# Layer 3 of a graph network: 22 full steps from up to two chunks each, instead of 42 steps of one chunk

## The chip, the core and the metric

The kernel runs on one core of one Trainium2 chip. The metric is the time on the device in microseconds (us), the median of several executions. A core has TensorE (PE; matmuls, results go to banks of PSUM memory), VectorE (DVE), ScalarE (ACT; functions such as exp and ln), GpSimd (POOL; here it issues the gathers) and SyncE (SP; here it issues the plain loads), and 16 DMA engines[...]. Each engine runs its own instructions in a fixed order, and waits on semaphores for those of the others.

## The reference

Four graph layers on 2708 nodes with 128 features and a dense 0/1 matrix adj of 2708 x 2708. Each layer is x = x + layer(relu(layernorm(x)), adj). The change concerns the fourth:

```python
def _L3_gnn_ref(X, A, W, a):
    XW = jnp.matmul(X, W)
    f = W.shape[1]
    s_col = jnp.matmul(XW, a[0, :f])
    s_row = jnp.matmul(XW, a[0, f:])
    Z1 = jax.nn.leaky_relu(s_row[:, None] + s_col[None, :], negative_slope=0.01)
    den = jnp.exp(Z1)
    num = jnp.matmul(A, den)
    att = jnp.where(num != 0, den / jnp.where(num != 0, num, 1.0), 0.0)
    H = jnp.matmul(A, jnp.matmul(att, XW))
    return H
```

So num is a product of two 2708 x 2708 matrices, of which the second, den, is built from one number for each row (r = s_row) and one for each column (c = s_col).

## The kernel before

Layers 0 to 2 stream the adjacency matrix through TensorE in 22 tiles of 128 rows (the rows of the page with line L209). They end at about 443 us and the change leaves them alone. Everything is float32 unless noted; a float32 matmul shows in the trace as two records.

Layer 3 doesn't form num by a full product. It sorts the nodes by r and cuts them into NC = 22 chunks of CH = 126 nodes. A column with the value c meets the bend of the leaky relu, r + c = 0, inside one chunk. For the nodes of all lower chunks and of all higher ones the leaky relu is linear, so their exp factors into a number of the node and one of the column: two prefix sums over the sorted nodes stand for them. num of one column is therefore a sum over 128 terms: the 126 nodes of its chunk and two prefix rows. The columns are grouped by their chunk, and one step takes up to 128 columns of one chunk. As each chunk's count is rounded up to full steps, the loop has a fixed NS = (2708 + 22 x 127) // 128 = 42 steps (L425), many with few columns or none.

**The tables** (L501 to L772, about 443 to 589 us) are built on the chip, since they depend on the data. First the rank of each node (L555 to L602). Then:

- sums(t) (L626): prefix sums of the adjacency. adj_t is streamed in 22 tiles of 128 rows into the four buffers of the pool steps (tag rows); the first two tiles go into dflat. Six matmuls a tile (L635). Its result goes through hn to a table pre_d in device memory (L778 to L786).
- ktab (L655 to L662): for each chunk the r and the number of its nodes, by a one-hot matmul.
- many (L684 to L688): how many columns each chunk has; pre (L674): how many columns of the same chunk come before each column.
- place, pos, step, slot (L697 to L709): the step of each column and its place in it. ohp and jrhs are the one-hot factors of the matmul L716, which collects, for each step, c (c_tab), the node number (xw_i) and exp(c) (c_exp).
- sel and pick (L732 to L747): for each step its chunk, hence which rows of adj_t (row_i) and of pre_d (pre_i) to gather, and r_step.
- densities(s0) (L749), for four steps at a time: dmat, the 128 x 128 matrix exp(leaky(r + c)) of each step. TensorE spreads c over the partitions (L761), VectorE adds r and applies the slopes, ScalarE the exp. dmat lies in dflat.

**The loop** (L808 to L826). fetch(s) (L793) gathers the 126 rows of the chunk from adj_t and two rows from pre_d into one of the four buffers of steps, and the projected features of the step's columns (fetch_xw, L457) into one of four xw_s. All gathers are issued by POOL, in order. Then, for each of six blocks b of up to 512 nodes, L817 computes num for 128 columns into a PSUM bank (there are two, L83), ScalarE takes its Ln (L818), VectorE subtracts it (L820) from e, which L813 set to the exponent of den without its linear part. After the six blocks ScalarE takes the exp of e (L822): this is att, but for factors of the row and the column. spread_values(s - 1) (L803) then multiplies the step before: six matmuls L806 of xw and e, collected over all steps in six PSUM banks. e and ln have two buffers (L788). Ln and exp need different ACT tables, so that each step shows two table loads.

**What sets the order.** The Tile framework schedules: [...] work may stand earlier than where the code has it. A pool's buffer is handed out again when its last reader is done.

After the loop the result is turned and scaled (L829 to L836), and a last product with adj_t (L860) ends the kernel; it streams adj_t into the buffers of steps and three more.

## Time and profile before

| | us |
|---|---|
| median of 3 runs | 1143.9 (1142.64 to 1145.51) |
| the profiled execution, as run | 1146.82 |
| its span, first to last instruction | 1145.0 |
| layers 0 to 2 | 0 to about 443 |
| tables of layer 3 | about 443 to 613 |
| loop, first L817 to last L806 | 613.32 to 1035.04 |
| last product | 1035.9 to the end |
| busy: PE, DVE, ACT, POOL | 1058.6, 557.5, 587.8, 260.0 |
| mean granted TensorE clock | 0.972 of full speed |

The page lists groups of instructions by line, engine, operation and tiles. The busy share of an engine is a mean over stages with different limits; what an edit is worth is read in its own stage. The chain of waits follows the last instruction back to what released it. In the timeline, each row gives the start, the duration, the engine, the line, the operation, and in brackets the idle time before it and what ended it. Both kernels print the same way, so the stages can be laid side by side.

### The profile page before, as it was taken

How to read it: one execution, taken by the hardware profiler on the slowest of the kernel's cores; microseconds unless marked ns; L12 is line 12 of the kernel's file. 1: busy time of each engine (PE TensorE's matmuls, PEld its weight loads, DVE VectorE, ACT ScalarE, POOL GpSimd, SP SyncE). 2: the span in 40 equal slices, each digit the busy share in tenths (PEclk: the TensorE clock that was granted, in tenths of full speed). 3: DMA queues.
4: the chain of work that ended last, by engine and by line, in shares of the span. 5: the costliest groups of instructions: out<-in, count | busy, mean ns of one | idle time of the engine just before them, and what ended most of it. 6: DMA issues, size and time to landing. Idle time of an engine off the chain costs nothing.

```text
span 1145.0 us, 8681 instructions
## 1 busy us (share of the span) xinstructions
PE 1058.6 (92%) x3110; PEld 464.3 (41%) x3110; DVE 557.5 (49%) x910; ACT 587.8 (51%) x682; POOL 260.0 (23%) x172
## 2 busy tenths in 40 slices
PE   5799999999999997759985999999999999999998
PEld 3333333444545444424421344444444444445444
DVE  5899999410131014884953455545554445542001
ACT  4689673210040003670014888888888888880000
POOL 3000001100110001100212455555555555500000
PEclk9899999999999998888998999999999999999999
DMA  8165544488647805302985344444444444647851
GB/s 320 68 250 212 188 158 125 158 302 304 223 195 260 309 14 209 134 1 107 369 316 188 129 150 153 152 153 152 145 139 140 144 147 152 188 159 317 306 210 48
DMA packets 36684, 211.64 MB, mean 185 GB/s; under 512 B 8234, under 2 KB 17114, under 8 KB 17874
## 3 DMA queue, kind: packets, MB, share of 16 engines
q1 hardware_dynamic: 21223, 146.96, 34.5%
q0 software_dynamic: 9408, 61.00, 16.2%
q10 hardware_dynamic: 6011, 3.14, 1.1%
q8 instruction: 24, 0.39, 0.1%
q14 instruction: 18, 0.15, 0.0%
HBM read 207.77 MB, written 3.32 MB: 184 GB/s over the span
## 4 chain that ended last, share of the span: by engine, by line
PE 28%; ACT 23%; DMA 2%; DVE 1%; issue 1%; DVEq 0%; POOLq 0%
PE bank L817 11%; PE acc L209 9%; ACT e L822 9%; ACT ln L818 6%; ACT L818 4%; ACT L822 4%; PE acc L635 4%; DMA rows<-in_adj_t_dram 2%; PE acc L806 1%; PE bank L761 1%; PE bank L185 1%; PE acc L660 0%; PE acc L716 0%; DMA xw<-xw_d,xw_i 0%; DVE e L820 0%
## 5 line engine op out<-in xcount | busy, mean ns | idle before, releaser
L817 PE MATMUL bank<-rows,dflat 128*128 128x512 f32 x504 | 218.8, 564 | 25.7 <-ACT ln L818 16.0
L806 PE MATMUL acc<-e,xw 128*128 128x512 f32 x504 | 198.0, 542 | 2.1 <-ACT e L822 2.1
L820 DVE TENSOR_TENSOR e<-e,ln 128x1536 f32<-128x1536 f32 (+2 forms) x126 | 134.6, 1097 | 109.4 <-ACT ln L818 104.9
L818 ACT ACTIVATE ln<-bank,tiny 128x512 f32<-128x512 f32 x252 | 151.5, 634 | 57.7 <-PE bank L817 57.2
L817 PEld LDWEIGHTS bank<-rows,dflat 128*128 128x128 f32 x504 | 83.3, 190 | 157.8 <-ACT ln L818 118.0
L450 POOL DMA_INDIRECT xw<-xw_d,xw_i x42 | 90.6, 2157 | 238.6 <-PE acc L806 150.7
L806 PEld LDWEIGHTS acc<-e,xw 128*128 128x128 f32 x504 | 93.0, 190 | 103.1 <-issue 90.4
L813 DVE TENSOR_SCALAR e<-row_a,c_rel 128x2708 f32<-128x2708 f32 x42 | 68.5, 1630 | 99.9 <-PE acc L806 99.8
L822 ACT ACTIVATE e<-e 128x2708 f32<-128x2708 f32 x42 | 103.3, 2460 | 1.7 <-DVE e L820 1.2
L209 PE MATMUL acc<-rows,hn 128*128 128x512 f32 (+1 forms) x264 | 101.7, 542 | 0.0
L209 PE MATMUL acc<-a,hn 128*128 128x512 f32 (+1 forms) x264 | 100.9, 542 | 0.0
L204 ACT COPY yT<-acc 128x512 f32<-128x512 f32 x9 | 5.2, 581 | 178.4 <-PE acc L209 174.9
L450 POOL DMA_INDIRECT rows<-pre_d,pre_i x42 | 89.9, 2140 | 29.7 <-DMA pre_d<-hn 17.2
L209 PE MATMUL acc<-a,hs 128*128 128x512 f32 (+1 forms) x228 | 88.1, 542 | 0.0
L286 ACT ACTIVATE tau<-row_a,e_neg,e_lo 128x1536 f32<-128x1536 f32 (+1 forms) x44 | 65.0, 1509 | 36.5 <-PE bank L301 26.6
L301 PE MATMUL bank<-tau,pick 128*6 128x512 f32 x180 | 72.6, 542 | 0.0
L209 PEld LDWEIGHTS acc<-a,hn 128*128 128x128 f32 x264 | 47.0, 190 | 50.2 <-issue 50.2
L209 PEld LDWEIGHTS acc<-rows,hn 128*128 128x128 f32 x264 | 46.8, 190 | 49.0 <-issue 48.8
L209 PE MATMUL acc<-yT,hs 128*128 128x512 f32 x132 | 57.2, 571 | 7.8 <-DVE yT L292 7.8
L289 DVE SCALAR_TENSOR_TENSOR tau<-tau,e_hi,a 128x1536 f32<-128x1536 f32 (+1 forms) x38 | 60.5, 1622 | 3.0 <-ACT tau L286 3.0
L209 PEld LDWEIGHTS acc<-a,hs 128*128 128x128 f32 x228 | 41.2, 190 | 45.4 <-issue 45.4
L635 PE MATMUL acc<-rows,wts 128*44 128x452 f32 (+1 forms) x240 | 55.0, 581 | 3.7 <-DMA rows<-in_adj_t_dram 3.7
(263 smaller groups left out, 1056.4 us busy)
## 6 DMA issues: line engine op xcount, KB each, us to landing
rows<-in_adj_t_dram SPq DMA_DIRECT2D x40, 1354.0 KB, 7.5
a<-in_adj_dram SPq DMA_DIRECT2D x38, 1354.0 KB, 6.4
a<-in_adj_t_dram SPq DMA_DIRECT2D x21, 1354.0 KB, 6.2
keep<-in_adj_dram SPq DMA_DIRECT2D x2, 1354.0 KB, 5.7
dflat<-in_adj_t_dram SPq DMA_DIRECT2D x2, 1354.0 KB
xw_d<-hs ACTq DMA_DIRECT2D x1, 1408.0 KB
row_a<-rdeg_d ACTq DMA_DIRECT2D x1, 1354.0 KB
xs<-in_x_dram SPq DMA_DIRECT2D x5, 256.0 KB
```

The lines of the kernel that those rows point to most:

```text
L209: nc.tensor.matmul(accs[b][:, : hi - lo], stationary, moving[:, lo:hi], start=start, stop=stop)
L286: nc.scalar.activation(tau[:, :w], row_a[:, h0:h1], AF.Relu, bias=e_neg[:, t : t + 1], scale=e_lo[:, t : t + 1])
L289: nc.vector.scalar_tensor_tensor(tau[:, :w], tau[:, :w], e_hi[:, t : t + 1], a[:, h0:h1], ALU.add, ALU.mult)
L301: nc.tensor.matmul(den[: len(E0), : hi - lo], pick[:, b, :], tau[:, lo - h0 : hi - h0], start=(ndone == 0), stop=(t == T - 1 and b == NB - 1),
L450: return nc.gpsimd.indirect_dma_start(out=out, out_offset=None, in_=src, in_offset=bass.IndirectOffsetOnAxis(ap=idx, axis=0),)
L635: nc.tensor.matmul(accs[b][64 * h : 64 * h + 2 * NC, : hi - lo], wts[:, t, :], a[:, lo:hi], start=(t == 0), stop=(t == T - 1),)
L806: nc.tensor.matmul(accs[b][:, : hi - lo], xw, e[:, lo:hi], start=(s == 0), stop=(s == NS - 1))
L813: nc.vector.tensor_scalar(e, row_a[:, :N], c_rel[:, s : s + 1], 0.0, ALU.add, ALU.max)
L817: nc.tensor.matmul(num[:, : hi - lo], dmat[:, s, :], a[:, lo:hi], start=True, stop=True)
L818: nc.scalar.activation(ln[:, lo:hi], num[:, : hi - lo], AF.Ln, bias=tiny)
L820: nc.vector.tensor_sub(e[:, beg:hi], e[:, beg:hi], ln[:, beg:hi])
L822: nc.scalar.activation(e, e, AF.Exp)
```

## The change

The columns are packed into NE = 22 steps which are all full (128 x 22 = 2816 places for 2708 columns), and a step takes columns from up to two chunks: one that has a step of its own, and one taken from a row in which the columns of the large chunks are laid end to end. So each step needs two row sets, and num is the sum of two matmuls into the same bank, one for each chunk. Where a column isn't of the chunk, its density is made zero: its c in c_two is -3.0e4, and exp gives 0. The table code gets the packing: which chunks are small or large (donor), in which order they come (key, order), and where their columns go (shift_b, past). It is all on VectorE, on rows of 22 or tables of 22 x 22 elements (row, gathered, sums_before). There are now 44 dmat matrices (NS = 2 NE), for which dflat grows, but 22 columns in the tables of steps. krhs moves to yT and sel to hT, many is computed ahead of pre, and one more column block (chunk1) goes through the one-hot matmul. The loop runs 22 times: two fetches, one fetch_xw, 12 matmuls L817, the same six Ln, one exp and six matmuls L806 as before. The pools are as they were: four buffers for rows, two banks, two of e.

In the changed file the lines of the loop move: L716 becomes L809, L761 becomes L875, L817 becomes L933, L806 becomes L918, L818 becomes L936, L822 becomes L940.

```diff
--- before.py
+++ after.py
@@ -420,9 +420,16 @@
     CH = P - 2
     NC = T
-    NS = (N + NC * (P - 1)) // P
+    NE = T
+    NS = 2 * NE
     c_col, r_col = hs[:, :, P], hs[:, :, P + 1]
     xw_d = dram.tile([NPAD, D], F32, name="xw_d")
@@ -436,14 +443,14 @@
         pools.append(pools.pop(0))
         return fill(pool.tile([P, N], F32, tag="rows", name="rows"), src, t)
-    dflat = keepers.tile([P, 2 * N], F32, name="dflat")
+    dflat = keepers.tile([P, max(2 * N, NS * P)], F32, name="dflat")
     dmat = dflat[:, : NS * P].rearrange("p (s q) -> p s q", q=P)
...
@@ -652,7 +659,7 @@
...
-        krhs = tab.tile([P, T, 2 * NC], F32, tag="w1", name="krhs")
+        krhs = yT[:, : T * 2 * NC].rearrange("p (t b) -> p t b", b=2 * NC)
         nc.vector.tensor_mul(krhs[:, :, :NC], ohc, over(r_of, NC))
         nc.vector.tensor_mul(krhs[:, :, NC:], ohc, over(node_v, NC))
         p = acc_bank(3)
@@ -671,6 +678,11 @@
         nc.vector.memset(gej[:, :, NC], 0.0)
         nc.vector.tensor_tensor(gej[:, :, 1:NC], over(negc, NC - 1), along(edges[:, 1:], NC - 1), ALU.is_ge)
         ohb = tt("ohb", [P, T, NC], gej[:, :, :NC], gej[:, :, 1:], ALU.subtract, BF16)
+        p = acc_bank(3)
+        for t in range(T):
+            nc.tensor.matmul(p[:, :NC], ones_b, ohb[:, t, :], start=(t == 0), stop=(t == T - 1))
+        many = tab.tile([P, NC], F32, name="many")
+        nc.vector.tensor_copy(many, p[:, :NC])
         pre = acc_bank(5)
         nc.tensor.matmul(pre[:, : T * NC], before, ohb.rearrange("p t b -> p (t b)"), start=True, stop=False)
         for t in range(T - 1):
@@ -681,70 +693,172 @@
                 start=False,
                 stop=(t == T - 2),
             )
-        p = acc_bank(3)
-        for t in range(T):
-            nc.tensor.matmul(p[:, :NC], ones_b, ohb[:, t, :], start=(t == 0), stop=(t == T - 1))
-        many = tab.tile([P, NC], F32, name="many")
-        nc.vector.tensor_copy(many, p[:, :NC])
...
+        def row(name, n=NC):
+            return tab.tile([P, n], F32, name=name)
+        def square(x):
+            return x[:, :, None].to_broadcast([P, NC, NC])
+        def square_t(x):
+            return x[:, None, :].to_broadcast([P, NC, NC])
+        def gathered(name, m, x):
+            v = tt("sq_v", [P, NC, NC], m, square_t(x), ALU.mult, tag="w3")
+            o = row(name)
+            nc.vector.tensor_reduce(o, v, AX.X, ALU.add)
+            return o
+        def sums_before(name, x):
+            o = row(name)
+            nc.vector.tensor_tensor_scan(o, ones[:, :NC], x, 0.0, ALU.mult, ALU.add)
+            nc.vector.tensor_sub(o, o, x)
+            return o
...
+        d_key = sums_before("d_key", d_over)
+        s_key = sums_before("s_key", s_over)
+        d_idx = sums_before("d_idx", donor)
+        head = row("head")
+        nc.vector.scalar_tensor_tensor(head, d_idx, 0.0, donor, ALU.is_equal, ALU.mult)
...
+        key = row("key")
+        nc.vector.tensor_mul(key, d_key, donor)
+        nc.vector.tensor_sub(key, key, head)
...
+        n_row = row("n_row")
+        nc.vector.tensor_mul(n_row, many, inrow)
+        n_own = row("n_own")
+        nc.vector.tensor_sub(n_own, many, n_row)
+        nc.vector.scalar_tensor_tensor(key, key, 2.0, donor, ALU.mult, ALU.add)
+        nc.vector.scalar_tensor_tensor(key, key, 32.0, lane[:, :NC], ALU.mult, ALU.add)
+        ahead = tt("ahead", [P, NC, NC], square(key), square_t(key), ALU.is_gt, tag="ohc")
+        order = row("order")
+        nc.vector.tensor_reduce(order, ahead, AX.X, ALU.add)
+        row_beg = gathered("row_beg", ahead, n_row)
+        own_before = gathered("own_before", ahead, n_own)
+        far_down = float(1 << 16)
+        own_beg = row("own_beg")
+        nc.vector.tensor_scalar(own_beg, order, -1.0, float(P), ALU.add, ALU.mult)
+        row_at = row("row_at")
+        nc.vector.tensor_sub(row_at, own_beg, own_before)
...
         place = tt(
-            "place", [P, T, NC], pre[:, : T * NC].rearrange("p (t b) -> p t b", b=NC), along(s_off, NC), ALU.add, tag="w3")
...
+        at = row("at", T)
+        nc.vector.tensor_reduce(at, place, AX.X, ALU.add)
+        past = tt("past", [P, T, NC], over(at, NC), along(row_at, NC), ALU.is_ge, tag="w3")
+        nc.vector.tensor_mul(past, past, along(n_own, NC))
+        pos = row("pos", T)
+        nc.vector.tensor_reduce(pos, past, AX.X, ALU.add)
...
+        chunk1 = row("chunk1", T)
+        nc.vector.tensor_reduce(chunk1, gej[:, :, :NC], AX.X, ALU.add)
+        gs = tt("gs", [P, T, NE + 1], over(pos, NE + 1), along(by_p, NE + 1), ALU.is_ge, tag="w1")
+        ohst = tt("ohst", [P, T, NE], gs[:, :, :NE], gs[:, :, 1:], ALU.subtract, tag="w2")
+        step = row("step", T)
         nc.vector.tensor_reduce(step, gs[:, :, 1:], AX.X, ALU.add)
...
         nc.vector.tensor_tensor(ohp, along(lane, P), over(slot, P), ALU.is_equal)
-        jrhs = row_b[:, : T * 3 * NS].rearrange("p (t s) -> p t s", s=3 * NS)
-        nc.vector.tensor_mul(jrhs[:, :, :NS], ohst, over(c_col, NS))
-        nc.vector.tensor_mul(jrhs[:, :, NS : 2 * NS], ohst, over(node_v, NS))
-        nc.vector.tensor_mul(jrhs[:, :, 2 * NS :], ohst, over(w_col, NS))
+        jrhs = row_b[:, : T * 4 * NE].rearrange("p (t s) -> p t s", s=4 * NE)
+        for i, v in enumerate((c_col, node_v, w_col, chunk1)):
+            nc.vector.tensor_mul(jrhs[:, :, i * NE : (i + 1) * NE], ohst, over(v, NE))
         p = acc_bank(4)
         for t in range(T):
-            nc.tensor.matmul(p[:, : 3 * NS], ohp[:, t, :], jrhs[:, t, :], start=(t == 0), stop=(t == T - 1))
...
+        c_chunk = row("c_chunk", NE)
+        nc.vector.tensor_copy(c_chunk, p[:, 3 * NE : 4 * NE])
         nc.vector.tensor_scalar_mul(c_rel, c_tab, -0.99)
         for s in range(3):
             fetch_xw(s)
...
-        sel = tt("sel", [P, NS, NC], steps_by(lane[:, :NS]), chunks_by(s_beg), ALU.is_ge, tag="w1")
-        sel_e = tt("sel_e", [P, NS, NC], steps_by(lane[:, :NS]), chunks_by(s_end), ALU.is_ge, tag="w2")
-        nc.vector.tensor_sub(sel, sel, sel_e)
+        sel = hT[:, : NS * NC].rearrange("p (e h b) -> p e h b", h=2, b=NC)
+        sel_v = hT[:, NS * NC : 2 * NS * NC].rearrange("p (e h b) -> p e h b", h=2, b=NC)
+        nc.vector.tensor_tensor(sel[:, :, 1, :], square(lane[:, 1 : NE + 1]), square_t(order), ALU.is_equal)
+        early = tt("early", [P, NE, NC], square(lane[:, :NE]), square_t(order), ALU.is_ge, tag="w3")
+        nc.vector.tensor_mul(early, early, square_t(n_own))
+        at_e = row("at_e")
+        nc.vector.tensor_reduce(at_e, early, AX.X, ALU.add)
+        nc.vector.scalar_tensor_tensor(at_e, lane[:, :NE], float(P), at_e, ALU.mult, ALU.subtract)
...
+        nc.vector.tensor_tensor(sel[:, :, 0, :], square(at_e), square_t(row_beg), ALU.is_ge)
+        nc.vector.tensor_tensor(sel_v[:, :, 0, :], square(at_e), square_t(row_end), ALU.is_ge)
+        nc.vector.tensor_sub(sel[:, :, 0, :], sel[:, :, 0, :], sel_v[:, :, 0, :])
         def pick(name, x):
-            nc.vector.tensor_mul(sel_e, sel, chunks_by(x))
-            o = tab.tile([P, NS], F32, name=name)
-            nc.vector.tensor_reduce(o, sel_e, AX.X, ALU.add)
+            nc.vector.tensor_mul(sel_v, sel, x[:, None, None, :].to_broadcast([P, NE, 2, NC]))
+            o = tab.tile([P, NE, 2], F32, name=name)
+            nc.vector.tensor_reduce(o, sel_v, AX.X, ALU.add)
             return o
-        nc.vector.tensor_copy(row_i, pick("row_f", ktab[:, NC:]))
+        nc.vector.tensor_copy(row_i, pick("row_f", ktab[:, NC:]).rearrange("p e h -> p (e h)"))
         chunk = pick("chunk", lane[:, :NC])
         up = tab.tile([P, 1], F32, name="up")
         nc.vector.tensor_scalar_mul(up, part, float(NC))
...
-        r_step = pick("r_step", ktab[:, :NC])
+        nc.vector.tensor_scalar(pre_i, chunk.rearrange("p e h -> p (e h)"), up, None, ALU.add)
+        r_step = pick("r_step", ktab[:, :NC]).rearrange("p e h -> p (e h)")
+        second = tab.tile([P, NE], F32, name="second")
+        nc.vector.tensor_reduce(second, sel[:, :, 1, :], AX.X, ALU.add)
+        nc.vector.tensor_add(second, second, chunk[:, :, 1])
+        nc.vector.tensor_tensor(second, second, c_chunk, ALU.is_equal)
+        c_two = tab.tile([P, NE, 2], F32, name="c_two")
+        gone = row("gone")
+        nc.vector.tensor_mul(gone, c_tab, second)
+        nc.vector.tensor_sub(c_two[:, :, 0], c_tab, gone)
+        nc.vector.scalar_tensor_tensor(c_two[:, :, 0], second, -3.0e4, c_two[:, :, 0], ALU.mult, ALU.add)
+        nc.vector.tensor_scalar(second, second, -1.0, 3.0e4, ALU.add, ALU.mult)
+        nc.vector.tensor_add(c_two[:, :, 1], gone, second)
+        c_two = c_two.rearrange("p e h -> p (e h)")
         def densities(s0):
             n = min(4, NS - s0)
@@ -754,7 +868,7 @@
             nc.vector.tensor_tensor(
                 diag[:, :n],
                 ident[:, None, :].to_broadcast([P, n, P]),
-                c_tab[:, s0 : s0 + n, None].to_broadcast([P, n, P]),
+                c_two[:, s0 : s0 + n, None].to_broadcast([P, n, P]),
                 ALU.mult,
             )
             p = bank()
@@ -796,17 +910,18 @@
             gather(a[CH:, :], pre_d[:, :], pre_i[0:2, s : s + 1])
             if 0 < s < 4:
                 tc.keep_in_program_order(one)
-            if s >= 3:
-                fetch_xw(s)
-            return a, xw_s[s % 4]
+            return a
         def spread_values(s):
             xw, e = done.pop(s)
             for b, (lo, hi) in enumerate(E0):
-                nc.tensor.matmul(accs[b][:, : hi - lo], xw, e[:, lo:hi], start=(s == 0), stop=(s == NS - 1))
-        for s in range(NS):
-            a, xw = fetch(s)
+                nc.tensor.matmul(accs[b][:, : hi - lo], xw, e[:, lo:hi], start=(s == 0), stop=(s == NE - 1))
+        for s in range(NE):
+            a2 = [fetch(2 * s + h) for h in range(2)]
+            if s >= 3:
+                fetch_xw(s)
+            xw = xw_s[s % 4]
             nc.vector.tensor_scalar_mul(xw, xw, c_exp[:, s : s + 1])
             e = attp.tile([P, N], F32, tag="e", name="e")
             ln = attp.tile([P, N], F32, tag="ln", name="ln")
@@ -814,7 +929,10 @@
             beg = 0
             for b, (lo, hi) in enumerate(E0):
                 num = bank()
-                nc.tensor.matmul(num[:, : hi - lo], dmat[:, s, :], a[:, lo:hi], start=True, stop=True)
+                for h in range(2):
+                    nc.tensor.matmul(
+                        num[:, : hi - lo], dmat[:, 2 * s + h, :], a2[h][:, lo:hi], start=(h == 0), stop=(h == 1)
+                    )
                 nc.scalar.activation(ln[:, lo:hi], num[:, : hi - lo], AF.Ln, bias=tiny)
                 if b in (2, 4, 5):
                     nc.vector.tensor_sub(e[:, beg:hi], e[:, beg:hi], ln[:, beg:hi])
@@ -823,7 +941,7 @@
             done[s] = (xw, e)
             if s:
                 spread_values(s - 1)
-        spread_values(NS - 1)
+        spread_values(NE - 1)
     scale = small.tile([P, T], F32, tag="scale", name="scale")
```

## The prediction

> **What bounds the kernel now.** First the page, for its costliest groups: columns are busy us and mean ns, then the engine's idle time before the group and what ended it. A matmul of the program shows as two records, so x504 is 6 for each of 42 steps.
>
> ```profile
> L817 PE MATMUL bank<-rows,dflat 128*128 128x512 f32 x504 | 218.8, 564 | 25.7 <-ACT ln L818 16.0
> L806 PE MATMUL acc<-e,xw 128*128 128x512 f32 x504 | 198.0, 542 | 2.1 <-ACT e L822 2.1
> L818 ACT ACTIVATE ln<-bank,tiny 128x512 f32<-128x512 f32 x252 | 151.5, 634 | 57.7 <-PE bank L817 57.2
> L822 ACT ACTIVATE e<-e 128x2708 f32<-128x2708 f32 x42 | 103.3, 2460 | 1.7 <-DVE e L820 1.2
> ```
>
> The loop is 37% of the span, nearly all of it TensorE. Next the timeline of one steady step (start, duration).
>
> ```profile
> 708.88 0.96 ACT L818 ACTIVATE ln<-bank,tiny 128x512 f32<-128x512 f32 x2 [0.36 <-PE bank L817]
> 708.93 4.71 PE L806 MATMUL acc<-e,xw 128*128 128x512 f32 x12
> ...
> 709.86 1.28 ACT L822 ACT_TABLE_LOAD   x1
> 711.15 2.46 ACT L822 ACTIVATE e<-e 128x2708 f32<-128x2708 f32 x1
> 713.47 1.88 PE L817 MATMUL bank<-rows,dflat 128*128 128x512 f32 x4
> 713.63 1.28 ACT L818 ACT_TABLE_LOAD   x1
> ...
> 715.66 3.28 PE L817 MATMUL bank<-rows,dflat 128*128 128x512 f32 x8 [0.31 <-ACT ln L818]
> ```
>
> A step starts every 9.86 us. The six acc matmuls take 713.47 - 708.93 = 4.54 us; TensorE idles 0.3 us. The exp (with its table load, until 713.61) lies under acc matmuls, because those use the step before: in this order acc(s) comes after all of num(s+1). Only the loop's first step shows acc reaching its exp too soon:
>
> ```profile
> 620.92 1.98 PE L817 MATMUL bank<-rows,dflat 128*128 128x512 f32 x4 [0.53 <-ACT ln L818]
> ...
> 622.46 2.46 ACT L822 ACTIVATE e<-e 128x2708 f32<-128x2708 f32 x1
> ...
> 624.97 1.12 PE L806 MATMUL acc<-e,xw 128*128 128x512 f32 x2 [2.06 <-ACT e L822]
> ```
>
> Then the chain of waits, for the ends of the stage: the sums stage waits for streamed rows before the loop, and the loop's last matmul ends at 1035.04.
>
> ```profile
> 587.11 10.13 DMA rows<-in_adj_t_dram
> 597.28 5.59 PE acc L635 x20
> ...
> 1030.23 4.81 PE acc L806 x12
> ```
>
> Last TensorE's granted clock in stretches of 3.41 us (columns: us, PE busy and records, clock, DMA share, GB/s).
>
> ```profile
> 593.67:597.08 3.41, 1.28 (x8) 1.00 0.87 238
> 597.08:600.49 3.41, 3.21 (x10) 0.50 0.62 194
> ...
> 620.97:624.39 3.42, 1.94 (x4) 1.00 0.93 355
> 624.39:627.80 3.41, 1.96 (x4) 1.00 1.04 286
> ```
>
> A stretch with 38% work is followed by one at half clock, 57% work is not.
>
> [...] the trace shows that a window need not be idle throughout: 1.28 us of work did not save it. [...] the exp starts 0.01 us after its load. [...] the 128x484 multiplies at L464 and L699 show 0.66.
>
> **The change part by part.** All against the profiled span of 1145.0 us; the run of it was 1146.8, the median of the runs 1143.9, so the difference is laid on the median.
>
> *The steady step.* It has 12 num matmuls and 6 acc matmuls: at 4.54 us per six (2708 columns), 3 x 4.54 = 13.6 us of TensorE. ACT stays at 8.6 us a step, covered. But the emitted TensorE order changes: num(s), the first block of num(s+1), then acc(s), where before it was num(s+1) entire. So acc(s) meets its own exp in every step. From the end of num(s), T: before, exp ended 713.61 - 708.93 = 4.68 us after T. The last block's two matmuls of 148 columns give Ln of the block before it 0.25 us more start, so I take 4.5. The cover is one block, 2 x 0.86 us, which waits some 0.3 us for Ln to free its bank: done at T + 2.0. TensorE then idles 2.5 us. After acc (4.54), five blocks remain: 2196 columns x 2 at 1.68 ns = 7.4. Step: 4.5 + 4.54 + 7.4 = 16.4 us.
>
> *The clock.* An idle 2.5 us falls into one 3.41-us window or is split over two; when one window has over about half idle (bounds from above: 43% safe, 62% not), the next runs at half clock, under busy acc and num matmuls, and costs up to 1.7 us: 18.1 us. Five windows are 17.07 us. A 16.4-us step moves the stall 0.6 us earlier on the grid, one of 18.1 us 1.0 us later: it drifts until the two alternate, so I take 17.1 as mean. Bounds: 16.4 (never dropped), 18.1 (always).
>
> *Gathers.* Four row buffers are now two steps. Both fetches of step s+2 wait for num(s), and POOL issues rows 0.97, pre 0.88 to 2.35, twice, with 0.3 us between and xw 2.23 behind: the second rows is issued about 3.9 us after T. Rows land 7.2 us after issue (DMA table), so at about T + 11 to 13; they are needed at T + 16.4 or later. Volume 2.77 MB in 17.1 us is 162 GB/s; 355 was moved at the loop's start. Cost nothing; if the cover goes, the step becomes the gather time.
>
> *The loop's ends.* POOL's order is unchanged: rows 1 is gathered behind pre 0 and pre 1 (612.49, against num's start at 613.32). Before, it was for step 1; now step 0's second matmul needs it, at about 619.7. The start runs at half clock (610.7 to 617.5 showed 0.5) and with TensorE idle stays so to about 624.4: from 619.7 on, 8.2 us of num(0) take 10.6, end 630.3, 17.0 after the first num. Then 21 steps to the end of the last num, 4.5 + 4.6 for its exp and acc: 17.0 + 21 x 17.1 + 9.1 = 385.2. Before: 1035.04 - 613.32 = 421.7. Loop: -36.5. I add 0.7 for half a window under the last acc.
>
> *The table stage.* VectorE chain from the copy of many to the step matmuls (L716 before, L809 after): before 535.98 to 550.07, 14.1 us. Now many comes 2.4 us earlier, since its 22 matmuls go ahead of pre's. The order shows 25 instructions of 484 or 506 elements (pitch 0.58 free, 0.70 when it needs the one before; I take 0.60), one of 2816 (3.0) and 42 small ones (pitch 0.09 to 0.22; 0.13): 15 + 3 + 5.5 = 23.5, from 533.6 to 557.2, 7 us late. Behind the step matmuls (5.2) come three picks of 968 elements (2 x 1.15 each), and now four xw scalings ahead of c_two, which wait for xw gathers: 4.1 us each to land, the fourth 11 us after c_tab as before. Densities thus start at about 575.5 where L754's first group met its sum at 562.8, some 13 late; they take 11 groups of 2.5 us, VectorE bound, last matmul near 601 (584.66 before). TensorE order leaves 27 sums matmuls behind it, at 0.39 to 0.46 us: 11 to 12 us, ending near 613, where the sums ended at 603.6 before, held by row loads for 10.1 us. That wait is the cover which hides part of it: +10 us. Bounds: +3 (loads still decide), +18 (nothing hidden, cold clock).
>
> *Tail.* After the last acc the order is the same: 0.
>
> *Sum.* -36.5 + 0.7 + 10 = -25.8; 1143.9 - 25.8 = 1118.
>
> **Rivals.** *A, forecast*: 1118. Own range: step 16.4 gives another -14 (1104), 18.1 gives +21 (1139); table and start move it by -7 to +8, together 1095 to 1145. *B, no stall*: if exp is ready at acc, the step is 13.7 and the loop 17.0 + 21 x 13.7 + 9.1 = 313.8: -107.9 + 10, 1046. For it: TensorE work is then the only bound; against it: the order, and the 2.06-us wait shown at 624.97. *C, slower: the pair of gathers cannot land within a step*, two buffers a step being no slack. The step is then the time from num(s)'s end to the second landing. It decides above (421.7 - 10.7 - 26.1)/21 = 18.3 us. For it: POOL's pre gathers stretch from 0.88 to 2.35 us, the first four pairs kept DMA at 0.9 for 17 us; against: 7.2 us a landing when one is in flight. At 19.5 us: 17.0 + 409.5 + 9.1 - 421.7 + 10.7 = +24.6, 1168. *D, nothing to see*: clock dropped every step plus a table stage of +15: -15.5 + 0.7 + 15, about 0: 1144.
>
> **How the numbers follow.** A 0.76, B 0.06, C 0.13, D 0.05. Time 1118. Range 1092 to 1146: it holds A and D; B and most of C, under 0.2, are left out. No change is within 0.3% (3.4 us), which the measurement can just tell. Faster: A but 0.02 of it, and B: 0.80. Same: those 0.02, D's middle 0.03 and 0.01 of C: 0.06. Slower: C and the rest of D: 0.14.
>
> **What would show it.** Right: 21 waits of acc for exp of about 2.5 us each, half-clock windows in about half of the steps, a step of about 17 us, the first num's second matmul waiting for rows until 6 us after the first, L809 some 7 us late and sums ended 10 us late. Wrong: num waiting for DMA rows in steady steps (C), a step under 15 us (B), or a steady clock of 1.00 with steps of 16.4.

## The result, and the profile after

The changed kernel takes 1157.6 us (median of 4 runs, 1152.6 to 1160.1), against 1143.8 before: the ratio is 1.0114, with a 95% interval of 1.0077 to 1.0151. The forecast was 1118 us, faster. The sign was wrong.

The profiled execution has a span of 1156.9 us against 1145.0, so 11.9 us have to be found. Three stretches share them as follows:

| stretch (us) | before | after | difference | forecast |
|---|---|---|---|---|
| start to the first num matmul | 613.32 | 625.06 | +11.7 | +10 |
| loop, first num to end of last acc | 421.72 | 421.86 | +0.1 | -35.8 |
| end of loop to end of span | 109.96 | 109.98 | 0.0 | 0 |

The last column is the sum of the prediction, whose loop was -36.5 + 0.7. The table stage came within 2 us and the tail was right. The whole error is in the loop, which gained nothing although it has 20 acc fewer.

The page of the changed kernel, its costliest groups (busy time, mean ns of one, idle time of the engine before it and what ended it):

```profile
L933 PE MATMUL bank<-rows,dflat 128*128 128x512 f32 (+1 forms) x528 | 218.1, 557 | 44.6 <-ACT ln L936 31.7
L918 PE MATMUL acc<-e,xw 128*128 128x512 f32 (+1 forms) x264 | 125.4, 631 | 47.0 <-ACT e L940 47.0
```

These are the two lines that were L817 and L806. The acc records fell from 504 to 264 as intended, but their mean rose from 542 to 631 ns, and idle time before them from 2.1 to 47.0 us. Before num it rose from 25.7 to 44.6, most of it now for Ln. The stretch view of the loop sums it up (us, then busy time and records of each engine, granted clock, DMA share, GB/s). The kernel before:

```profile
613.32:1035.04 421.72, 403.61 (x1010) 171.27 (x1011) 208.13 (x206) 362.67 (x380) 211.53 (x119) 0.99 0.47 154
```

The changed kernel:

```profile
625.06:1046.92 421.86, 339.73 (x794) 147.63 (x795) 107.98 (x106) 191.23 (x201) 96.83 (x103) 0.94 0.45 158
```

TensorE is busy 63.9 us less and idle 64.0 us more (421.86 - 339.73 = 82.1 against 18.1). So the work did go away. What it left behind is idle time, and part of the rest runs at a lower clock. The idle time is accounted for by the groups: 47.0 us before acc for exp, 31.7 before num for Ln, and 3.4 for rows 1 at the start.

The timeline of one step and a half, TensorE and the ScalarE instructions that it waits for (start, duration, then the instruction and the idle time before it):

```profile
705.79 5.92 PE L933 MATMUL bank<-rows,dflat 128*128 128x512 f32 x16 [1.26 <-ACT ln L936]
...
711.99 1.98 PE L933 MATMUL bank<-rows,dflat 128*128 128x512 f32 x4 [0.27 <-ACT ln L936]
...
713.52 2.46 ACT L940 ACTIVATE e<-e 128x2708 f32<-128x2708 f32 x1
...
716.03 6.51 PE L918 MATMUL acc<-e,xw 128*128 128x512 f32 x12 [2.06 <-ACT e L940]
...
722.38 1.88 PE L933 MATMUL bank<-rows,dflat 128*128 128x512 f32 x4
...
723.48 1.28 ACT L936 ACT_TABLE_LOAD   x1 [7.50 <-PE bank L933]
...
724.78 1.26 ACT L936 ACTIVATE ln<-bank,tiny 128x512 f32<-128x512 f32 x2
...
725.52 5.92 PE L933 MATMUL bank<-rows,dflat 128*128 128x512 f32 x16 [1.26 <-ACT ln L936]
...
731.71 1.98 PE L933 MATMUL bank<-rows,dflat 128*128 128x512 f32 x4 [0.27 <-ACT ln L936]
...
735.76 4.81 PE L918 MATMUL acc<-e,xw 128*128 128x512 f32 x12 [2.06 <-ACT e L940]
```

Read it from 711.99. Two num matmuls (four records) stand ahead of acc, and acc waits 2.06 us for its own exp, both as forecast. Then come two more num matmuls at 722.38, and only at 723.48 can ScalarE load Ln's table: it has stood 7.50 us for a num bank. Had block 0 been complete at 713.97, when those four records end, that Ln could have run under acc. It was not complete. In the emitted order the two matmuls ahead of acc write two different banks and both read the rows of the first chunk: they are the first halves of blocks 0 and 1, and their second halves come behind acc. The lines above agree: ScalarE is released by the first of the two matmuls at 722.38, and then has two Ln to do at once (x2 at 724.78). Why the scheduler parted the halves is not shown. So nothing of Ln lies under acc, and TensorE stands another 1.26 us for it before block 2.

The 21 steps, from exp to exp, take 393.3 us, where 21 x 17.1 = 359.1 was forecast. The first is 15.58 us; of the other twenty, ten are 18.02 or 18.03 and ten are 19.72 or 19.73 (one of these 20.02), 18.89 on the mean. The two lengths differ by the acc of 6.51 against 4.81 us above.

### The profile page after: what moved, and what is told of

The parts are those of the page before. It is cut to its first block, busy times and chain, and to the rows that moved or that the text cites. A ratio compares the mean times of both kernels' runs of the same rounds, so it can differ in the third digit from the quotient of the medians.

```text
span 1156.9 us, 8034 instructions
## 1 busy us (share of the span) xinstructions
PE 1000.5 (86%) x2894; PEld 445.8 (39%) x2894; DVE 469.0 (41%) x868; ACT 415.2 (36%) x502; POOL 143.5 (12%) x156
## 4 chain that ended last, share of the span: by engine, by line
PE 38%; ACT 13%; DVE 3%; DMA 1%; issue 1%; POOL 0%; ACTq 0%; POOLq 0%; DVEq 0%
PE bank L933 12%; PE acc L918 11%; PE acc L209 9%; ACT e L940 5%; PE acc L642 3%; ACT ln L936 3%; ACT L940 2%; ACT L936 2%; PE bank L875 1%; PE acc L809 1%; DMA rows<-in_adj_t_dram,row_i 1%; DMA xw<-xw_d,xw_i 1%; PE bank L185 0%; PE acc L667 0%; POOL xw L457 0%
## 5 line engine op out<-in xcount | busy, mean ns | idle before, releaser
L933 PE MATMUL bank<-rows,dflat 128*128 128x512 f32 (+1 forms) x528 | 218.1, 557 | 44.6 <-ACT ln L936 31.7
L918 PE MATMUL acc<-e,xw 128*128 128x512 f32 (+1 forms) x264 | 125.4, 631 | 47.0 <-ACT e L940 47.0
L933 PEld LDWEIGHTS bank<-rows,dflat 128*128 128x128 f32 x528 | 93.7, 192 | 155.2 <-issue 100.6
L938 DVE TENSOR_TENSOR e<-e,ln 128x1536 f32<-128x1536 f32 (+2 forms) x66 | 70.6, 1097 | 153.5 <-ACT ln L936 153.5
L936 ACT ACTIVATE ln<-bank,tiny 128x512 f32<-128x512 f32 x132 | 79.3, 634 | 81.7 <-PE bank L933 81.5
L918 PEld LDWEIGHTS acc<-e,xw 128*128 128x128 f32 x264 | 55.2, 216 | 129.3 <-ACT e L940 64.6
L928 DVE TENSOR_SCALAR e<-row_a,c_rel 128x2708 f32<-128x2708 f32 x22 | 35.9, 1630 | 157.0 <-PE acc L918 157.0
L286 ACT ACTIVATE tau<-row_a,e_neg,e_lo 128x1536 f32<-128x1536 f32 (+1 forms) x44 | 65.0, 1509 | 36.5 <-PE bank L301 26.6
L457 POOL DMA_INDIRECT rows<-in_adj_t_dram,row_i x44 | 42.4, 963 | 263.9 <-PE bank L933 256.7
L209 PE MATMUL acc<-row_b,hs 128*128 128x512 f32 x132 | 55.5, 553 | 0.0
L642 PE MATMUL acc<-rows,wts 128*44 128x452 f32 (+1 forms) x240 | 54.1, 574 | 1.2 <-DMA rows<-in_adj_t_dram 1.2
```

Of the source, the lines that this page charges most:

```text
L209: nc.tensor.matmul(accs[b][:, : hi - lo], stationary, moving[:, lo:hi], start=start, stop=stop)
L286: nc.scalar.activation(tau[:, :w], row_a[:, h0:h1], AF.Relu, bias=e_neg[:, t : t + 1], scale=e_lo[:, t : t + 1])
L457: return nc.gpsimd.indirect_dma_start(out=out, out_offset=None, in_=src, in_offset=bass.IndirectOffsetOnAxis(ap=idx, axis=0),)
L642: nc.tensor.matmul(accs[b][64 * h : 64 * h + 2 * NC, : hi - lo], wts[:, t, :], a[:, lo:hi], start=(t == 0), stop=(t == T - 1),)
L918: nc.tensor.matmul(accs[b][:, : hi - lo], xw, e[:, lo:hi], start=(s == 0), stop=(s == NE - 1))
L928: nc.vector.tensor_scalar(e, row_a[:, :N], c_rel[:, s : s + 1], 0.0, ALU.add, ALU.max)
```

## The experiments

Unless it is said otherwise, each is an edit of the changed kernel. The matmuls that an edit wraps in keep_in_program_order stand in the source order in the traces below (in e1, 24 records of num and then 12 of acc). The changed kernel wraps no matmul of the loop and leaves their order to the scheduler.

**e1: num whole, then acc of the step before.** The source order as written, with acc(s-1) behind all of num(s).

```diff
-                nc.tensor.matmul(accs[b][:, : hi - lo], xw, e[:, lo:hi], start=(s == 0), stop=(s == NE - 1))
+                tc.keep_in_program_order(nc.tensor.matmul(accs[b][:, : hi - lo], xw, e[:, lo:hi], start=(s == 0), stop=(s == NE - 1)))
...
-                    nc.tensor.matmul(
+                    tc.keep_in_program_order(nc.tensor.matmul(
                         num[:, : hi - lo], dmat[:, 2 * s + h, :], a2[h][:, lo:hi], start=(h == 0), stop=(h == 1)
-                    )
+                    ))
```

> Theory (the order on TensorE sets the step: acc(s-1) stands in the middle of num(s) and waits there for exp, and the rest of num(s) waits behind it): with num(s) whole ahead of acc(s-1), exp(s-1) has 9.4 us of num and is ready, no wait of L918 for exp and none of L933 for Ln is left, TensorE is never idle long enough for the clock to drop, and the step is TensorE's own work, 9.4 + 4.6, about 14 us; the loop is about 17.2 + 9.4 + 20 x 14.0 + 9.3 = 316 instead of 421.9, so about 1050 us. Rival 1 (two gathers of rows and two of pre cannot land within a step, four buffers being two steps): step 16 us or more, with L933 waiting for DMA rows; 1095 us or more. Rival 2 (ScalarE's two table loads a step bound it): L933 waits for Ln, step 15 to 18 us.

Measured: 1057.5 us (1056.3 to 1061.1), 0.9248 of before (0.9220 to 0.9276). Its groups and one step:

```profile
L933 PE MATMUL bank<-rows,dflat 128*128 128x512 f32 (+1 forms) x528 | 213.8, 555 | 25.2 <-ACT ln L936 10.9 <-DMA rows<-pre_d,pre_i 9.8 <-DMA rows<-in_adj_t_dram,row_i 4.5
L918 PE MATMUL acc<-e,xw 128*128 128x512 f32 (+1 forms) x264 | 103.4, 542 | 0.0
```

```profile
781.65 2.46 ACT L940 ACTIVATE e<-e 128x2708 f32<-128x2708 f32 x1
...
784.22 3.60 PE L933 MATMUL bank<-rows,dflat 128*128 128x512 f32 x8
...
786.18 1.28 ACT L936 ACT_TABLE_LOAD   x1 [2.07 <-PE bank L933]
...
788.21 5.92 PE L933 MATMUL bank<-rows,dflat 128*128 128x512 f32 x16 [0.40 <-ACT ln L936]
...
793.97 4.71 PE L918 MATMUL acc<-e,xw 128*128 128x512 f32 x12
```

The exp of 781.65 is used by the acc of 793.97: it has all of num to hide behind. No idle time is left before acc, its mean is back at 542 ns, and the clock is 1.00 from 700 to 900 us. The step is 14.30 us. The two DMA waits in the first line, 9.8 and 4.5 us, are those of the loop's start. In a step of 14.3 us nothing waits for a gather, which ends the rival in which a pair of gathers could not land within a step. The forecast of 1050 us was 7 us too low. 0.40 us a step is the wait for Ln that stands in the line above; the expectation had none.

**e2: the order that the prediction had assumed.** Both halves of block 0, then acc(s-1), then blocks 1 to 5, all pinned.

```diff
             for b, (lo, hi) in enumerate(E0):
                 num = bank()
...
+                if s and b == 0:
+                    spread_values(s - 1)
                 nc.scalar.activation(ln[:, lo:hi], num[:, : hi - lo], AF.Ln, bias=tiny)
...
-            if s:
-                spread_values(s - 1)
```

> This is the order that the prediction assumed: both halves of block 0 of num(s), then acc(s-1), then blocks 1 to 5. Theory (the sum of the prediction was right for that order and failed because in the changed kernel the two blocks ahead of acc are first halves only, so that no Ln can run under acc): the wait of 1.26 us for Ln after acc is gone, the undropped step is 16.4 to 16.6 us instead of 18.0, 18.1 to 18.3 where the clock drops, about 17.3 on the mean: 1125 us (1115 to 1140). Rival (the two halves don't matter, the step is held by something else, gathers or ScalarE): step still 18.0 and 19.7, 1155 to 1160 us.

Measured: 1120.9 us (1116.7 to 1124.9), ratio 0.9789 (0.9750 to 0.9828). One step:

```profile
763.53 1.98 PE L933 MATMUL bank<-rows,dflat 128*128 128x512 f32 x4 [0.27 <-ACT ln L938]
...
767.54 1.28 ACT L938 ACT_TABLE_LOAD   x1
767.58 4.81 PE L918 MATMUL acc<-e,xw 128*128 128x512 f32 x12 [2.06 <-ACT e L942]
...
768.84 0.69 ACT L938 ACTIVATE ln<-bank,tiny 128x512 f32<-128x512 f32 x1
772.22 7.53 PE L933 MATMUL bank<-rows,dflat 128*128 128x512 f32 x20
```

The table load and the Ln of block 0 now lie under acc (767.54 to 769.53), and five blocks follow without a wait. The steps are 16.50 us, and 18.20 in every third: 17.07 on the mean. The only change is which two halves stand ahead of acc: both of block 0, not one each of blocks 0 and 1. With that, the step and the total are those of the prediction within 0.3%, and the wait for exp is 2.06 us of the 2.5 that it gave.

**e3: the changed kernel's order, with the idle time filled.** The source now writes that order out, and two matmuls a step whose result is overwritten stand before acc.

```diff
+            half(0, 0)
+            if s:
...
+                for k in range(2):
+                    tc.keep_in_program_order(nc.tensor.matmul(
+                        nums[1][:, : hi - lo], dmat[:, 2 * s, :], a2[0][:, lo:hi], start=True, stop=True
+                    ))
+            half(1, 0)
+            if s:
+                spread_values(s - 1)
+            half(0, 1)
+            half(1, 1)
```

> The order of the changed kernel, with two repeated matmuls a step (their result is overwritten) put into the idle time before acc, 1.72 of 2.06 us. Theory (the steps of 19.7 us are those in which the clock drops to half after that idle time, 1.7 us each, in about half of the steps): the added work costs nothing, all steps are 18.0 to 18.2 us, clock 1.00 in the loop, 21 x 0.8 = 17 us less: about 1141 us. Rival (the slower acc has another cause than TensorE's idle time, the gathers that land meanwhile): 18.0 and 19.7 still alternate, 1155 to 1160 us. If the fill stands on the path: steps 19.7 throughout, 1175 us.

Measured: 1139.4 us (1137.8 to 1140.3), ratio 0.9953 (0.9935 to 0.9971): 18.2 us less than the changed kernel for 42 more matmuls. One step:

```profile
746.67 1.12 PE L934 MATMUL bank<-rows,dflat 128*128 128x512 f32 x2 [0.28 <-ACT ln L958]
747.63 1.88 PE L942 MATMUL bank<-rows,dflat 128*128 128x512 f32 x4
749.35 1.02 PE L934 MATMUL bank<-rows,dflat 128*128 128x512 f32 x2
750.72 4.81 PE L918 MATMUL acc<-e,xw 128*128 128x512 f32 x12 [0.35 <-ACT e L962]
```

L942 is the filling. All steady steps but one (18.32) are 18.02 or 18.03 us, none 19.72, and the clock is 1.00 from 700 to 900 us, where the changed kernel had 0.95. So the slower acc comes from the idle time ahead of it and not from the gathers that land meanwhile. And the order alone, at full clock, gives a step of 18.02 us: the halves as read from the changed kernel, written out by hand, have its step.

**e4: the four xw scalings behind the densities.** On VectorE they stood ahead of c_two and waited for xw's gathers.

```diff
-            nc.vector.tensor_scalar_mul(xw, xw, c_exp[:, s : s + 1])
+            scaled = nc.vector.tensor_scalar_mul(xw, xw, c_exp[:, s : s + 1])
+            if s < 4:
+                tc.keep_in_program_order(scaled)
```

> Only the four xw scalings of steps 0 to 3 are moved behind the densities on VectorE. Theory (of the 11.7 us that the loop starts later, a part is VectorE standing in front of these scalings for xw's gathers, 1.4 + 3.4 + 0.8 us, ahead of the densities): the densities begin 4 to 5.5 us earlier, the sums end 3 to 5 us earlier and so does the loop's start; 1152 to 1155 us. Rival (row loads or TensorE's clock hold the sums): the densities begin earlier and the sums end where they did, 1157 us.

Measured: 1150.6 us (12 runs, 1145.0 to 1154.8), ratio 1.0049 (1.0028 to 1.0071); the median is 6.9 us below the changed kernel's, and the slowest of its runs overlap with the fastest of those. What went away is in the changed kernel's VectorE timeline:

```profile
565.74 0.18 DVE L811 COPY c_tab<-acc 128x22 f32<-128x22 f32 x1 [5.69 <-PE acc L809]
...
569.89 0.31 DVE L925 TENSOR_SCALAR xw<-xw,c_exp 128x128 f32<-128x128 f32 x1 [1.36 <-DMA xw<-xw_d,xw_i]
...
574.91 0.29 DVE L925 TENSOR_SCALAR xw<-xw,c_exp 128x128 f32<-128x128 f32 x1 [3.39 <-DMA xw<-xw_d,xw_i]
...
577.45 0.29 DVE L925 TENSOR_SCALAR xw<-xw,c_exp 128x128 f32<-128x128 f32 x1 [0.80 <-DMA xw<-xw_d,xw_i]
...
578.51 1.29 DVE L868 TENSOR_TENSOR diag<-ident,c_two 128x512 f32<-128x512 f32 x2
```

In e4 the first diag is at 571.81 and the loop starts at 618.36 instead of 625.06. So these waits are on the path, and hold the loop's start by 5.9 us, a little more than expected (of the 6.7 between the two starts, 0.8 is that the execution ran earlier as a whole: many is copied at 533.01 instead of 533.78).

**e5: Ln's table loaded ahead.** e1 with a 128x1 Ln behind each exp, and the order on ScalarE pinned.

```diff
-            nc.scalar.activation(e, e, AF.Exp)
+            tc.keep_in_program_order(nc.scalar.activation(e, e, AF.Exp))
+            if s < NE - 1:
+                tc.keep_in_program_order(nc.scalar.activation(spare, tiny, AF.Ln, bias=tiny))
```

> e1_acc_behind with one 128x1 Ln (result unused) behind every exp, so that ScalarE loads Ln's table under the next block 0. Theory (what is left above TensorE's own work is the wait of 0.40 us for Ln in every step, since the table load waits with the Ln that needs it): the wait goes, step 13.9 instead of 14.3, 20 x 0.4 = 8 us less than e1_acc_behind: 1049 us. Rival (the next wait takes its place, two banks for num being too few): step stays 14.3, 1057 us.

Measured: 1048.2 us (1047.2 to 1048.8), ratio 0.9167 (0.9137 to 0.9197), 9.3 us less than e1.

```profile
753.85 1.28 ACT L943 ACT_TABLE_LOAD   x1
753.94 9.25 PE L934 MATMUL bank<-rows,dflat 128*128 128x512 f32 x24
...
763.03 4.71 PE L919 MATMUL acc<-e,xw 128*128 128x512 f32 x12
```

The load starts with block 0, and not, as at 786.18 in e1, when the first bank of num is done; num has 24 records without a gap, and the step is 13.63 us, less than the 13.9 expected. Now the step is TensorE's own work. With this order two banks for num are enough.

**e6: rows 1 gathered ahead of the two pre gathers**, on e1.

```diff
-            gather(a[CH:, :], pre_d[:, :], pre_i[0:2, s : s + 1])
-            if 0 < s < 4:
+            if s < 4:
                 tc.keep_in_program_order(one)
+            if s:
+                if s == 1:
+                    first = gather(held[0][CH:, :], pre_d[:, :], pre_i[0:2, 0:1])
+                    tc.keep_in_program_order(first)
+                two = gather(a[CH:, :], pre_d[:, :], pre_i[0:2, s : s + 1])
+                if s == 1:
+                    tc.keep_in_program_order(two)
```

> e1_acc_behind with the gather of rows 1 ahead of the two pre gathers that wait for pre_d. Theory (at the loop's start num(0) stands 4.5 us for rows 1, only because POOL issues it behind those waits): no wait for rows 1 is left, num(0) ends 4 to 6.5 us earlier, 1051 to 1053 us. Rival (rows 1 and pre 0 share the DMA engines, so the first num starts later by as much): 1057 us.

Measured: 1056.8 us (1052.4 to 1060.8) against 1057.5: no difference that these runs can tell. Num(0) no longer waits for rows 1, but the first num waits longer for pre:

```profile
627.86 11.82 PE L941 MATMUL bank<-rows,dflat 128*128 128x512 f32 x24 [14.81 <-DMA rows<-pre_d,pre_i]
```

In e1 that wait was 9.85 us. Here the wait grew by 5.0 and the one removed was 4.5. This fits the rival, that rows 1 and pre_d share the DMA engines; but see e11.

**e8: one matmul of 22x484 in the gap before L809**, on the changed kernel.

```diff
             nc.vector.tensor_mul(jrhs[:, :, i * NE : (i + 1) * NE], ohst, over(v, NE))
+            if i == 1:
+                p = acc_bank(4)
+                nc.tensor.matmul(
+                    p[:NE, : T * NE].rearrange("p (t s) -> p t s", s=NE), jrhs[:, 0, :NE], jrhs[:, :, NE : 2 * NE],
+                    start=True, stop=True,
+                )
```

> The changed kernel with one more matmul of 22x484 (result overwritten) on TensorE in the stretch before the step matmuls L809, where it has idle time of 2.3 us. Theory (L809 takes 9.5 us instead of 5.2 because the clock drops after that stretch): the clock stays at 1.00, L809 takes 5.2 us, c_tab comes about 4 us earlier; of that the loop's start gets 0 to 4 us: 1153 to 1158 us. Rival (L809 is slower for its operands or the wider tile): 9.5 us again.

Measured: 1154.0 us (1152.3 to 1154.7), ratio 1.0088 (1.0057 to 1.0118). TensorE's timeline of the changed kernel at L809:

```profile
556.21 9.49 PE L809 MATMUL acc<-row_b,yT 128*128 128x88 f32 x44 [2.30 <-DVE row_b L806]
```

And in e8, where L809 is the added matmul and the same 44 records are on line 814:

```profile
551.65 0.99 PE L809 MATMUL acc<-row_b 128*22 128x484 f32 x2 [1.56 <-DVE row_b L806]
552.57 2.48 PE L642 MATMUL acc<-rows,wts 128*44 128x452 f32 x12
555.79 5.14 PE L814 MATMUL acc<-row_b,yT 128*128 128x88 f32 x44 [0.74 <-DVE row_b L806]
```

The added matmul parts the gap: TensorE stands 1.56 and 0.74 us where it stood 2.30 in one piece. The 44 records then take 5.14 us at a clock of 1.00, instead of 9.49 with the clock at 0.50 from 556.46 on, and the loop starts at 620.91 instead of 625.06. Of those 4.2 us, 0.4 is that the execution ran earlier from before the added matmul on. The total fell by 3.5 us, with runs that overlap.

**e9: the kernel before, with e1's order pinned.** The same two edits, in the loop of 42 steps.

> The kernel before with the order of e1_acc_behind: num(s) whole, then acc(s-1), 42 steps of one chunk. Theory (before, TensorE's own work of 4.6 + 4.6 us already filled nearly all of a step of 9.86 us, so that the new order has little to win there, and what e1_acc_behind gained it could gain only because the change took 20 acc of 4.6 us out of the loop): step 9.3 to 9.9 us, 1121 to 1146 us. Rival (the order alone explains the gain, whatever the chunks in a step): step below 9 us, about 1060 us.

Measured: 1143.1 us (2 runs) against 1144.8 for before, ratio 0.9981 (0.9952 to 1.0009); the step is 9.85 us in nearly all of the loop, as before. But this is no test of the order. The kernel before already ran so: the prediction's timeline of a steady step has twelve num records from one acc to the next. e9 changes the order at the loop's start alone, and shows only that pinning in itself brings nothing that can be told. What answers the question is e1 against before, since both have this order in their steady steps and, beside the pinning, differ in the change alone. The loop of e1:

```profile
620.59:946.53 325.94, 310.57 (x794) 141.90 (x795) 108.06 (x106) 191.40 (x201) 115.28 (x103) 0.98 0.57 204
```

It is 95.8 us shorter than the 421.72 of before, where the 20 acc that the change takes out are 92 us. In the changed kernel's own order nothing of this was left.

**e7, e10 and e11: the parts together.** e7 is e1 with the edits of e4, e5 and e6; e10 adds that of e8; e11 is e7 without that of e6.

> e1_acc_behind, e4_scale_late, e5_ln_ahead and e6_rows1_ahead together. If their gains lie in different stretches and add: 1057 - 5 - 8 - 5 = 1039 us. If the earlier start of the loop only makes it wait for pre_d or the gathers: 1045 to 1050 us.

> e7_all with the filling matmul of e8_table_fill. If the two gains in the table stage add: 1037 - 4 = 1033 us. If, with the scalings out of the way, another wait (row loads) ends the sums: 1037 us.

> e7_all without the earlier gather of rows 1, which alone brought nothing in e6_rows1_ahead. If it is worth nothing here too: 1037 us, with a wait of num(0) for rows 1 that the later landing of pre 0 paid for. If it is worth what num(0) waits for rows 1: 1041 to 1043 us.

Measured: e7 1036.9 us (1030.8 to 1037.7), ratio 0.9052 (0.9011 to 0.9093); e10 1031.9 us (1029.7 to 1033.7), ratio 0.9009 (0.8987 to 0.9030); e11 1040.4 us (1036.6 to 1043.5), ratio 0.9083 (0.9053 to 0.9112). The gains add: e11 is 17.0 us below e1, where e4 and e5 alone brought 6.9 + 9.3, and e10 is 5.0 below e7, where e8 alone brought 3.5. e10 is the fastest of all, 113 us below before. In its profiled execution the loop starts at 612.75, where before it started at 613.32: these edits repay the whole cost of the change in the table stage. For rows 1, e11 against e7 gives 3.6 us, but their runs overlap, and e6 against e1 gave 0.6; what the earlier gather is worth stays open.

## Why the prediction was wrong

**The steady step: wrong, and the cause of the wrong sign.** The step that failed is the reading of the order on TensorE, "num(s), the first block of num(s+1), then acc(s)". The count was right, two matmuls ahead of acc, but they are not one block. They are half of two. From this the prediction drew two things that don't hold: that "After acc (4.54), five blocks remain", and, since it put no wait for Ln behind acc, that Ln of the first block would be done by then. That wait is 1.26 us in every steady step. At full clock the step divides like this, from 698.01 to 716.03 in the changed kernel and from 767.58 on in e2:

| part | forecast | after | e2 |
|---|---|---|---|
| acc | 4.54 | 4.65 | 4.64 |
| acc's end to the next block 0 | 7.4 | 9.33 | 7.8 |
| the two num matmuls ahead of acc, and idle time | 4.5 | 4.04 | 4.05 |
| step | 16.4 | 18.02 | 16.50 |

The middle row is 3.13 (two second halves and 1.26 of wait) plus 6.20 us in the changed kernel. The forecast's own 16.4 is e2's 16.50. The 21 steps together took 393.3 - 359.1 = 34 us too long, of the 36 by which the loop missed; 20 x (18.02 - 16.4) = 32 of them are this step. The bounds of 16.4 and 18.1 for the step did not hold the truth because both ends assumed the same order; only the clock was varied.

**The wait for exp: right.** "TensorE then idles 2.5 us" is 2.06 + 0.27 in the trace, in every steady step.

**The clock: right in the changed kernel.** The forecast put 0.7 us a step on it and let the two lengths alternate; the twenty steps show 18.89 - 18.02 = 0.87. e3 takes this away, 20 x 0.87 = 17 us, and its total fell by 18.2. In the order that was forecast (e2) the mean is 17.07 against 17.1, but there one step in three is slow and not every other.

**The gathers: right.** No wait for rows after the loop's start, in steps of 18 us as forecast, and none in 13.63 us either (e5). The point from which the slower rival was to decide, a step of 18.3 us, was itself sound: the step became 18.73, and the kernel slower. Only it was TensorE's order that brought it there and not the DMA.

**The loop's start: right in sum.** Num(0) ends at 642.06, 17.0 us after the first num, as forecast. In it the wait for rows 1 is 3.44 us, not 6, since two first halves are done before it.

**The table stage: right within 2 us, one term mis-sized.** VectorE's chain reaches L809 at 556.21 (557.2). The "step matmuls (5.2)" took 9.49: behind an idle 2.30 us nearly all of them ran at a clock of 0.50, and in e8, where that idle time is parted, all ran at 1.00. The waits of the xw scalings were in the sum (the fourth 11 us after c_tab; 11.7), and e4 shows that they are on the path. Sums end at 615.6 (613).

**The rivals.** "B, no stall" gave 1046 us for a loop with no wait for exp. e1 is that loop, at 1057.5 us, and e5, without its 0.40-us wait, 1048.2. Its price was right, and its mechanism needs an order that the changed kernel doesn't have. "D" assumed the clock dropped in every step and a table stage of +15; the trace has half of the steps and +11.7. The range given for "A", 1095 to 1145, is 2 us too low by its own terms (1118 - 14 - 7 and 1118 + 21 + 8); nothing hangs on it.

So the expected gain was real, and was lost where it was made. The loop lost 20 x 4.6 = 92 us of acc, and TensorE's busy time fell by only 63.9. By estimate, num's 24 more records took about 9 us of the rest, and the dropped clock 10 x 1.7 = 17 in the steps and a few more at the loop's ends. Those 63.9 then went into waits: idle time in the loop rose by 64.0.

## What to carry to other kernels

When a sum over two operands is split into start and stop matmuls, a scheduler may put the halves of one tile on both sides of other work. Follow each matmul's bank and operand in the emitted order, not the number of matmuls, to see when a tile is complete and its reader can start. An engine that must wait for a result of its own last work wants a whole piece of other work in between: here num of the next step (9.3 us) hides the exp (4.3 us), two half blocks (1.7 us) do not. A wait of 2.06 us on TensorE cost 1.7 us more in the work behind it in half of the steps here, so fill such a wait or remove it.

## What the runs showed of the hardware

In the changed kernel the granted clock steps between 1.00 and 0.50, and the steps lie whole multiples of 3.413 us apart: it falls at 716.89, is back at 720.30, and falls at 1020.68 again, 89 times 3.413 us after the first fall. In the loop a window of that length that is only partly idle was enough for a fall. The trace in such windows, set so that they begin where the clock steps (us, TensorE busy and records, clock, DMA share, GB/s):

```profile
713.47:716.89 3.42, 1.36 (x4) 1.00 0.90 304
716.89:720.30 3.41, 3.41 (x5) 0.50 0.86 317
...
733.95:737.37 3.42, 1.61 (x4) 1.00 0.81 320
737.37:740.78 3.41, 3.41 (x10) 1.00 0.97 317
```

1.36 us of work in a window and the next one was at half clock; 1.61 us, and it was not. Over this loop each of the twelve windows at full clock that were busy for 0.40 to 1.40 us (41% or less) was followed by one at half clock, and none that was busy for 1.56 us (46%) or more. In e2, by estimate from its timelines, windows with 1.41 us of work kept the clock and those with 1.35 us lost it. So the border that these loops show lies near 1.4 us. The windows run on through the steps: in e2 two steps of 16.50 and one of 18.20 are 51.20 us, which is 15 windows of 3.413, and the pattern repeats from there.

Getting back was not the same for all work. Under an acc of 128x512 matmuls the clock was back at 1.00 after one window (716.89 to 720.30 above). Under the 44 records of L809, 88 columns each, it was not, although the trace shows TensorE busy throughout:

```profile
553.05:556.46 3.41, 1.11 (x8) 1.00 0.99 422
556.46:559.88 3.42, 3.42 (x18) 0.50 1.02 431
559.88:563.29 3.41, 3.41 (x18) 0.50 0.95 396
563.29:566.70 3.41, 3.41 (x16) 0.50 0.04 16
566.70:570.12 3.42, 3.42 (x20) 1.00 0.27 64
```

Three windows at half clock, until the wider L642 had begun at 565.63. In e8 the clock was 1.00 under the same 44 records, and stayed so in the windows behind them up to 569.77.

Nor does the busy share decide for every kind of work. The one-hot matmuls of ktab are 44 records of 44 columns. In the kernel before they fill a whole window (the first line here), and the clock dropped after it all the same; in the changed kernel, at 522.33, too:

```profile
521.99:525.40 3.41, 3.41 (x33) 1.00 0.00 0
525.40:528.81 3.41, 3.41 (x11) 0.50 0.00 0
```

At full clock the records of 44 columns (L667) start every 0.11 us, and those of 88 (L814 in e8, 44 in 5.14 us) every 0.12 us. From the 0.43 us that a record of 512 columns takes in steady flow one may estimate that columns stream for about a third of that time in the first and about two thirds in the second. This would fit that only the first lost the clock. It doesn't say why the records of 88 columns didn't bring it back. No run here tests either.
